# Eight banks of PSUM shared out anew in a fused attention and feed-forward kernel

## Chip, cores and metric

One core of one Trainium2 chip runs the whole program. The metric is the device time of one execution in microseconds (us); the time before is the median of three runs. A profile is one more execution, taken with the hardware profiler on.

## What is computed

Input is `x` of 128 sequences x 64 steps x 256 features (fp32), and one condition vector of 256 for each sequence. The reference, cut to what matters:

```python
# layer 0: a gated recurrence over the 64 steps, then a quantised feed-forward (256 -> 704 -> 256)
def step(h, z_t):
    gate = sigmoid(h @ Wh.T + z_t @ Wz.T + b)
    h_new = tanh(h * leak + gate * z_t)
    return h_new, h_new
...
h = _act_fake_quant(silu(gate) * up, clip_down[0])        # needs the largest |h| of all tokens
x = x + h @ _weight_fake_quant(w_down).T                  # "down projection"
# layer 1: a block in hyperbolic space with adaptive layer norm, 16 heads of 16
xn = layer_norm(logmap0(x));  xm = expmap0(xn * (1 + sc_msa) + sh_msa)
q, k, v = (_to_heads(plin(xm, w, b)) for w, b in ...)
attn = softmax(q k / sqrt(16))
attn_out = plin(_from_heads(expmap0(attn @ v)), w_o, b_o)
x2 = mobius_add(x, expmap0(g_msa * logmap0(attn_out)))
xn = layer_norm(logmap0(x2)); xm = expmap0(xn * (1 + sc_mlp) + sh_mlp)
ff = plin(plin(xm, w_f1, b_f1), w_f2, b_f2)               # "feed-forward"
y = mobius_add(x2, expmap0(g_mlp * logmap0(ff)))
# layer 1: a linear layer on values rounded to fp6 in blocks of 32
out = x + mx_quantize(y) @ mx_quantize(weight).T + bias   # "fp6 linear"
```

## The kernel before

The 8192 tokens are 64 tiles of 128 tokens; four tiles are a group, so there are 16 groups, and a group is worked on as two pairs of tiles.

Up to about 310 us the recurrence runs, then the wide half of the quantised feed-forward, whose result goes to DRAM because its scale needs the largest value of all tokens. From there on one fused part (`fused`) takes the groups through everything else. Its main loop issues, for a step `k`:

- `tail(k)`: the end of a residual step for the attention of group `k` and the feed-forward of group `k - LM` (LM = 3) together: `tail_coeffs` (from L745) is a chain of some 35 small VectorE (DVE) instructions on 128 x 8 numbers with powers on GpSimd (POOL, `rsqrt`, L632), then `combine` (L789).
- `norms(k)`: the layer norms for the feed-forward of group `k` and the attention of group `k + LA` (LA = 5) together: `ln_coeffs` (from L658) is a second chain of that kind, then `modulate` (L712 to L717), a sum of squares on ScalarE (ACT, L601), and `clip_ball` (L610, L612), which scales the result.
- `fp6(k - LM)`: rounding, transposition (`turn`, L92), copy to SBUF (L1077), product (L1081, L1083), sum with the residual (L1086).
- `mlp(k)`: transposition, a split in two parts (L1021, L1022), product in three passes (L1026, L1029), read out by DVE (L1032) and ACT (L1035), then L1041.
- `attention(k + LA)`: transposition and projection to q, k, v (`qk`, L905, L908, copied by L910), norms of the heads (L912 to L925), their scaling on POOL (L934, L938), transposition and scores (`sc`, L959), exponentials (L967), attention times values (`ao`, L974, read out by L978 and L979), transposition, copy (L995) and output projection (L1000, read out by L1004), then `tail_sums` (L601 and L729).
- `front(k + LA + 1)`: the down projection of layer 0 for a later group (`dn`, L872, read out by L874), sum with the input `xr` (L875), statistics for its norm (L695, L696).

TensorE (PE) writes only to PSUM, which has eight banks of 128 x 512 fp32 numbers. A tile of PSUM is a whole bank, and `bank(tag)` (L591) takes the next of the tag's buffers: 2 for `qk`, 2 for `sc`, 1 each for `ao`, `ml`, `fp`, `dn`, as CFG (L46) says. A tag with one buffer can be written again only when its last reader, on DVE or ACT, is done.

What stands in which order is not written out by hand. The program is built under

```python
    with _tile.TileContext(nc, schedule_with_timeline_sim=True) as tc:
```

so a planner takes the instructions as issued, with the loop's order as their priority, follows its own estimate of when operands and buffers become free, and lays down a queue for each engine. On the chip each engine works through its queue in that order and waits on semaphores. The functions marked `@first` (`radial`, `ln_coeffs`, `tail_coeffs`) have a higher priority. All loads and stores are issued from one queue, that of SyncE (SP, `move`, L567).

Of the kernel before, what the change touches and what calls it, by code (L numbers as in the profile page):

```python
# [11 lines left out]
F32 = mybir.dt.float32  # L12
# [10 lines left out]
P = 128  # L23
# [19 lines left out]
NG = NT // GN  # L43
AR = 8
TS = 4
CFG = {'rnd': 'S', 'ef': 8, 'fill': {'x1a': 'V', 'mod0': 'V'}, 'hold': [3, 0], 'mk': 3, 'mv': 6, 'xs': 3, 'la': 3, 'sb': 7, 'qks': 'GGGG', 'deq': 'VV', 'first': 1000, 'hb': 2, 'q_h': 'P', 'q_x1': 'P', 'q_xr': 'P', 'q_ot': 'P', 'q_out': 'P', 'q_ada': 'P', 'room': [[0.3, 0.3, 0.55], [0.5, 0.4, 0.2]], 'qv': 64, 'p1': 'GVGVGVGV', 'x1': 3, 'u1': 16, 'u2': 6, 'qkv': 2, 'sq': 1, 'uT1': 2, 'uT2': 2, 'qM': 2, 'kT': 2, 'e': 4, 'oT': 1, 'yT': 1, 'hq': 2, 'hl': 2, 'xr': 1, 'ot': 2, 'ada00': 2, 'ada02': 2, 'ada10': 2, 'ada12': 4, 'dn': 1, 'qk': 2, 'sc': 2, 'ao': 1, 'ml': 1, 'fp': 1, 'mod0': 'GGGV', 'mod1': 'VVVV', 'sqm0': 'SSSS', 'sqm1': 'SSSS', 'su0': 'VVVV', 'su1': 'VGVG', 'q8': 'GGGGGG', 'hqc': 'SSSVVV', 'qm': 'SSSS', 'x1a': 'GV', 'gate0': 'GGGG', 'gate1': 'GGGG', 'yb': 'GG', 'va': 'GGGG', 'sqt': 'SSSS', 'sqg': 'SSSS', 'sqo': 'SSVS', 'f2e': 'SSSS', 'early': 0, 'q8f': 'VVVVVV', 'hqf': 'SSSVVV', 'fl': 1, 'un': 2, 'jsu': 1, 'LA': 5, 'LM': 3, 'tl': 6, 'ord': 1, 'xt': 3, 'q_xt': 'P'}  # L46
GT = 4
NGR = NTILE // GT

LA, LM = CFG["LA"], CFG["LM"]  # L50

# [19 lines left out]
def tile_kernel(ctx, tc, a, out):  # L71
# [64 lines left out]
    with ExitStack() as l0:  # L136
# [15 lines left out]
        with ExitStack() as sc_:  # L152
# [260 lines left out]
            for n in range(T // TS):  # L413
# [5 lines left out]
                for i in range(TS):  # L419
# [22 lines left out]
                    with tc.issue_after(lv.ins), tc.issue_after(ls.ins), tc.issue_after(lp.ins):  # L442
                        next(ahead, None)
                        for q in range(2):
                            if t < CFG["hold"][q]:
                                continue
                            left[q] = [min(l, 0.0) + r for l, r in zip(left[q], CFG["room"][q])]
                            while min(left[q]) > 0:
# [25 lines left out]
        for b0 in range(0, B, NBB):  # L474
            for c in range(2):

                q8 = xp.tile([P, NBB, T], I8, name="q8", tag="q8")
                src = hsT[:, c, :, b0 : b0 + NBB].rearrange("p t b -> p b t")
                if b0 < CFG["qv"]:
                    V.tensor_scalar(q8, src, isx, None, ALU.mult)  # L480
# [16 lines left out]
        def h_chunk(pg, pu, j, at, dst):  # L497
# [3 lines left out]
            cnt[0] += 1  # L501
            if CFG["p1"][cnt[0] % 8] == "G":
                uv = fw.tile([P, GN], F32, name="uv", tag="uv")
# [39 lines left out]
def fused(ctx, tc, a, out_tok, x_tok, L):  # L543
    nc = tc.nc
    V, S, G_, PE = nc.vector, nc.scalar, nc.gpsimd, nc.tensor
# [10 lines left out]
    ps = ctx.enter_context(tc.tile_pool(name="fps", bufs=1, space=PSUM))  # L556
# [9 lines left out]
    def move(key, out, in_):  # L566
        Q[CFG["q_" + key]].dma_start(out=out, in_=in_)  # L567

# [19 lines left out]
            es = CFG["fill"].get(key, es)  # L588
        return es[g % len(es)]

    def bank(tag):  # L591
        return ps.tile([P, 512], F32, name=tag, tag=tag, bufs=CFG[tag])

    def big(tag, shape, dt=F32):
        return pl.tile(shape, dt, name=tag, tag=tag, bufs=CFG[tag])
# [248 lines left out]
    def front(i):  # L844
# [4 lines left out]
        for h2 in pairs:  # L849
            pr = i0 // 2 + h2  # L850
            early = pr < CFG["early"]
            grp = pr // 2
            hs_ = slice((grp % 2) * 64, (grp % 2) * 64 + 64)
            hl = hls.pop(0)
            hq = big("hq", [P, 6, 2 * P], BF16)
            q8 = big("hb", [P, 6, 2 * P], I8)

            for e, r, j in runs("q8f" if early else "q8", hs_):
                scale(e, q8[r, j, :], hl[r, j, :], cu[r])
            for e, r, j in runs("hqf" if early else "hqc", hs_):  # L860
                if e == "V":
                    V.tensor_copy(hq[r, j, :], q8[r, j, :])
                else:
                    S.copy(hq[r, j, :], q8[r, j, :])
            load_h(pr + CFG["hl"])
            xr = big("xr", [P, 2, D])
            move("xr", out=xr, in_=x_tok[:, i0 + 2 * h2 : i0 + 2 * h2 + 2, :])
            py = bank("dn")
            for i in range(2):
                for j in range(6):  # L870
                    r = slice(0, P) if j < 5 else hs_
                    PE.matmul(py[:, i * D : (i + 1) * D], lhsT=hq[r, j, i * P : (i + 1) * P], rhs=wdT[r, j, :],  # L872
                              start=(j == 0), stop=(j == 5))
            V.tensor_tensor(x1.t[h2], two(py), bc_out(sdh, 2), ALU.mult)  # L874
            ENG[pick("x1a", h2)].tensor_tensor(x1.t[h2], x1.t[h2], xr, ALU.add)  # L875
            for g in (2 * h2, 2 * h2 + 1):
                stats(mv1[:, g, :], x1[g], 1)
            move("x1", out=x1_d[:, i0 + 2 * h2 : i0 + 2 * h2 + 2, :], in_=x1.t[h2])

    def attention(i, u, sums):  # L880
# [4 lines left out]
        for h2 in pairs:  # L885
# [3 lines left out]

            uT = big("uT1", [P, 2, 2, 2 * P], F32R)  # L890
            pt = bank("qk")
            for c in range(2):
                po = pt[:, c * 256 : (c + 1) * 256].rearrange("p (s g t) -> p s g t", s=2, g=2)
# [5 lines left out]
            for xy in range(2):  # L899
                cs = slice(xy * P, (xy + 1) * P)  # L900
                for lo, hi in ((0, 512), (512, 768)):
                    pm = bank("qk")
                    n_ = hi - lo
                    o3 = slice(0, 3) if lo == 0 else slice(32, 35)
                    PE.matmul(pm[:, :n_], lhsT=ones3[o3, :], rhs=rows3[o3, :n_], start=True, stop=False)  # L905
                    for k in range(2):
                        for q, (w, z) in enumerate(PASSES):
                            PE.matmul(pm[:, :n_], lhsT=uT[:, z, k, cs], rhs=wqkv[:, w, k, lo:hi],  # L908
                                      start=False, stop=(k == 1 and q == 2))
                    S.copy(qkv[:, xy, lo:hi], pm[:, :n_])  # L910
                sq = big("sq", [P, 3 * D])
                S.activation(sq, qkv[:, xy, :], AF.Square)  # L912
                V.tensor_reduce(nh[:, xy * 48 : (xy + 1) * 48], sq.rearrange("p (h d) -> p h d", d=HD),  # L913
                                AX.X, ALU.add)
# [302 lines left out]
```

## Time and profile before

| | |
|---|---|
| runs of before | 1414.75, 1404.55, 1413.27 us: median 1413.27 |
| profiled execution | 1410.42 us, span 1408.5 us, granted clock 0.859 |
| busy, share of the span | PE 84%, DVE 81%, POOL 59%, ACT 58% |
| DMA | 163.64 MB, mean 116 GB/s |
| 300 to 420 us (fused part begins, attention of the first groups) | PE busy 78.3 of 120.0 us |
| 540 to 680 us | PE 129.7, DVE 121.5 of 140.0 us |
| 820 to 960 us | PE 120.7, DVE 129.7 of 140.0 us |
| 1300 to 1408.5 us (last groups run out) | PE 68.2, DVE 66.1 of 108.5 us |

The span is the time from the first to the last instruction. "Busy" is the time in which an engine has an instruction under way. "Granted clock" is the share of TensorE's full clock that the throttle lets through. Where a row shows "A <- B", A waited until B was done. Where a group of instructions is named, its name is that of the tile that is written and those that are read, without buffer numbers (`ao<-va,e`).

### The profile page before, as it was taken

Reading aid. Unit: us, or ns where it says so; the run is one execution under the profiler, and the core shown is the slowest. Engines: PE = TensorE matmul, PEld = TensorE weight load, DVE = VectorE, ACT = ScalarE, POOL = GpSimd, SP = SyncE. Lnnn points to the kernel's source line nnn. Section 1 sums busy time; section 2 is a strip of 40 time slices with the busy share of each in tenths; the row PEclk is TensorE's granted clock in tenths of the full one; section 3 lists DMA queues with packets and bytes.
Section 4 is the critical chain, followed back from the end, with each engine's and each line's share of the span. In section 5 each row is a group of like instructions: output and inputs, shape, how many; then the busy total and the mean of one; then the engine's idle time right before and its main releaser. Section 6 shows DMA issues by size and latency. Waiting matters only on the chain.

```text
span 1408.5 us, 23861 instructions
## 1 busy us (share of the span) xinstructions
PE 1183.5 (84%) x7372; PEld 748.0 (53%) x7380; DVE 1144.8 (81%) x3604; ACT 815.5 (58%) x2363; POOL 836.6 (59%) x1043
## 2 busy tenths in 40 slices
PE   7999977974699988999889988799996999785655
PEld 4656542322466655656556565556664666553433
DVE  5666669986687988979989789979889888788863
ACT  2545447972377766667656666667765756643331
POOL 3111108865688769776685776867758764645541
PEclk9999979985599987989879899889987969976675
DMA  7113145779534234341354231532314132222111
GB/s 230 53 53 92 59 198 206 273 253 301 166 118 127 94 103 134 109 135 46 101 151 146 81 115 43 158 116 77 102 39 136 49 119 68 82 73 93 60 45 45
DMA packets 119304, 163.64 MB, mean 116 GB/s; under 512 B 10885, under 2 KB 72074, under 8 KB 119178
## 3 DMA queue, kind: packets, MB, share of 16 engines
q1 hardware_dynamic: 119178, 162.13, 36.4%
q8 instruction: 58, 0.95, 0.3%
q14 instruction: 68, 0.56, 0.1%
HBM read 115.94 MB, written 46.14 MB: 115 GB/s over the span
## 4 chain that ended last, share of the span: by engine, by line
DVE 40%; PE 35%; POOL 10%; DMA 7%; ACT 4%; issue 4%; SPq 0%; POOLq 0%; DVEq 0%; ACTq 0%
DMA ada<-ada_d 4%; PE pg L426 4%; PE qk L908 4%; PE fp L1083 4%; DVE u L789 4%; PE pg L407 3%; PE sc L959 3%; PE ml L1029 2%; PE ao L974 2%; DVE nh L913 2%; DVE bn L695 2%; DVE u L716 2%; DVE junk L735 2%; DVE u L610 2%; DVE u L1041 2%
## 5 line engine op out<-in xcount | busy, mean ns | idle before, releaser
L601 ACT ACTIVATE junk<-u 128x256 bf16<-128x256 f32 x432 | 182.2, 424 | 143.0 <-DVE u L717 46.2
L908 PE MATMUL qk<-wqkv,uT 128*128 128x512 f32 (+1 forms) x768 | 199.4, 390 | 6.3 <-DVE uT L898 3.5
L729 POOL TENSOR_TENSOR u<-u,ada 128x256 f32<-128x256 f32 x128 | 101.1, 792 | 91.7 <-ACT junk L601 88.6
L908 PEld LDWEIGHTS qk<-wqkv,uT 128*128 128x128 f32 x768 | 129.9, 207 | 46.5 <-issue 12.4
L959 PE MATMUL sc<-qM,kT 64*64 64x256 f32 x1024 | 126.7, 437 | 9.7 <-ACT kT L949 6.1
L974 PE MATMUL ao<-va,e 128*64 128x34 f32 x2048 | 93.3, 248 | 35.4 <-DVE u L979 15.3
L1029 PE MATMUL ml<-wm,uT 128*128 128x512 f32 x384 | 122.6, 457 | 0.0
L974 PEld LDWEIGHTS ao<-va,e 128*64 128x64 f32 x2048 | 83.5, 163 | 62.5 <-issue 36.3
L608 ACT ACTIVATE qM<-sc,mhead 128x256 f32<-128x256 f32 x256 | 101.3, 492 | 21.3 <-PE sc L92 21.1
L872 PE MATMUL dn<-wdT,hq 128*128 128x256 bf16 (+1 forms) x384 | 72.3, 315 | 41.3 <-DVE x L874 16.5
L938 POOL TENSOR_TENSOR va<-qkv,comb 64x256 f32<-64x256 f32 x128 | 87.2, 682 | 30.1 <-PE ao L974 24.3
L1029 PEld LDWEIGHTS ml<-wm,uT 128*128 128x128 f32 x384 | 75.5, 212 | 53.5 <-issue 35.0
L505 POOL TENSOR_TENSOR hv<-uv,sil 128x512 f32<-128x512 f32 x44 | 57.4, 1308 | 70.8 <-DVE am L508 52.2
L1083 PE MATMUL fp<-wfT,yT 128*128 128x256 f32 x256 | 92.6, 491 | 0.0
L967 ACT ACTIVATE e<-sc 128x512 f32<-128x512 f32 x128 | 73.3, 596 | 24.5 <-PE sc L959 15.1
L910 ACT COPY qkv<-qk 128x512 f32<-128x512 f32 (+1 forms) x128 | 61.3, 498 | 44.4 <-PE qk L908 43.6
L601 ACT ACTIVATION_READ_ACCUMULATOR junk<-u 128x1 f32 x432 | 86.1, 199 | 0.0
L426 PE MATMUL pg<-hsT,WT 128*128 128x128 f32 x504 | 76.3, 292 | 10.8 <-ACT hsT L438 10.4
L934 POOL TENSOR_TENSOR qkv<-qkv,comb 128x512 f32<-128x512 f32 x64 | 70.4, 1117 | 23.7 <-DVE comb L925 9.3
L426 PEld LDWEIGHTS pg<-hsT,WT 128*128 128x128 f32 x504 | 66.1, 195 | 33.3 <-ACT hsT L438 31.1
L959 PEld LDWEIGHTS sc<-qM,kT 64*64 64x64 f32 x1024 | 55.5, 147 | 48.3 <-issue 17.3
L612 POOL TENSOR_SCALAR hb<-hl,cu 128x1280 int8<-128x1280 f32 x64 | 64.8, 1018 | 23.0 <-DMA hl<-h_d 14.3
(282 smaller groups left out, 3129.7 us busy)
## 6 DMA issues: line engine op xcount, KB each, us to landing
ada<-ada_d SPq DMA_DIRECT2D x128, 256.0 KB, 3.5
h_d<-hv SPq DMA_DIRECT2D x80, 256.0 KB, 2.1
hl<-h_d SPq DMA_DIRECT2D x32, 640.0 KB, 5.1
ada<-ada_d SPq DMA_DIRECT2D x128, 128.0 KB, 2.6
xt<-in_xT_dram SPq DMA_DIRECT2D x16, 512.0 KB, 4.1
xr<-in_x_dram SPq DMA_DIRECT2D x32, 256.0 KB, 3.7
x_d<-x SPq DMA_DIRECT2D x32, 256.0 KB, 2.4
xt<-x_d SPq DMA_DIRECT2D x32, 256.0 KB, 2.7
```

Source lines behind the costliest of these rows:

```text
L426: lp = PE.matmul(pg[c][:, st], lhsT=WT[:, k, c * P : (c + 1) * P], rhs=hp[:, k, :], start=False, stop=False, skip_group_check=True)
L601: S.activation(junk, src, AF.Square, accum_out=acc)
L608: S.activation(dst, src, AF.Copy, scale=by)
L729: ENG[pick(f"gate{which}", g)].tensor_tensor(av, av, gb, ALU.mult)
L872: PE.matmul(py[:, i * D : (i + 1) * D], lhsT=hq[r, j, i * P : (i + 1) * P], rhs=wdT[r, j, :], start=(j == 0), stop=(j == 5))
L908: PE.matmul(pm[:, :n_], lhsT=uT[:, z, k, cs], rhs=wqkv[:, w, k, lo:hi], start=False, stop=(k == 1 and q == 2))
L938: ENG[pick("va", g)].tensor_tensor(va[r, :, s, 0:HD], qkv[r, xy, 512:768].rearrange("p (h d) -> p h d", d=HD), bc_in(comb[r, xy * 48 + 32 ...
L959: PE.matmul(sc[rr][s * T : (s + 1) * T, c * 256 : (c + 1) * 256].rearrange("p (v t) -> p v t", v=4), lhsT=kTs[xy][r, c, s * T : (s + 1) * ...
L967: S.activation(e.rearrange("p c v t -> p (c v t)"), sc[rr], AF.Exp, scale=1.0 / math.sqrt(HD))
L974: PE.matmul(pv[xy * T : (xy + 1) * T, hh], lhsT=E[2 * xy + hh // 4][:, c, hh % 4, :], rhs=vas[(2 * h2 + xy) % 4][:, c * 8 + hh], start=Tru ...
L1029: PE.matmul(pm, lhsT=uT[:, z, k, i * P : (i + 1) * P], rhs=wm[:, w, k, :], start=False, stop=(k == 1 and q == 2))
L1083: PE.matmul(o, lhsT=yT[:, 2 * i + c, :], rhs=wfT[:, c, :], start=False, stop=(c == 1))
```

## The change

`ao` gets two buffers instead of one. The tags `ml`, `fp` and `dn` become one tag, `m`, with two buffers, which the three take in turn, in the order in which the planner places them. Eight banks are in use as before. The two added lines move the code below them by two lines; line numbers in this document are those of the kernel before.

```diff
-CFG = {... 'ada12': 4, 'dn': 1, 'qk': 2, 'sc': 2, 'ao': 1, 'ml': 1, 'fp': 1, 'mod0': 'GGGV', ...}
+CFG = {... 'ada12': 4, 'qk': 2, 'sc': 2, 'ao': 2, 'm': 2, 'mod0': 'GGGV', ...}
...
-    def bank(tag):
-        return ps.tile([P, 512], F32, name=tag, tag=tag, bufs=CFG[tag])
+    def bank(name):
+
+        tag = "m" if name in ("ml", "fp", "dn") else name
+        return ps.tile([P, 512], F32, name=name, tag=tag, bufs=CFG[tag])
```

## Prediction

> **What bounds the kernel now.** I read the page first: TensorE and VectorE carry almost the same load.
>
> ```profile
> PE 1183.5 (84%) x7372; PEld 748.0 (53%) x7380; DVE 1144.8 (81%) x3604; ACT 815.5 (58%) x2363; POOL 836.6 (59%) x1043
> ```
>
> Then I cut the fused part of the trace where one group's norm chain gives way to the next: L658 (`tln`) is the first instruction of `ln_coeffs`, it starts once per group, at 576.3 us for one group and at 1083.1 us for the one eight groups later. The stretches show span, then busy time (and instructions) of PE, PEld, DVE, ACT, POOL, then the granted clock.
>
> ```profile
> 312.00:576.30 264.30, 215.82 (x1551) 138.50 (x1552) 215.99 (x651) 156.07 (x427) 194.60 (x255) 0.81 0.49 147
> 576.30:1083.10 506.80, 446.67 (x3180) 297.26 (x3178) 449.58 (x1457) 323.89 (x995) 358.50 (x445) 0.89 0.35 106
> 1083.10:1408.50 325.40, 252.52 (x1417) 164.34 (x1415) 247.70 (x936) 157.16 (x496) 171.81 (x212) 0.77 0.22 69
> ```
>
> The middle stage takes 506.8 / 8 = 63.35 us a group, with PE at 88% and DVE at 89%: no engine has much room, and both must run beside each other all the time. How that is done shows when the middle stage is cut into the time from a group's L658 to its last scaling at L610 (the norm chain, after which `mlp` and `attention` of that group may begin):
>
> ```profile
> 662.50:725.70 63.20, 50.52 (x346) 33.37 (x342) 61.51 (x194) 38.13 (x116) 47.10 (x59) 0.89 0.43 129
> 704.00:764.00 60.00, 53.53 (x377) 35.52 (x377) 51.29 (x157) 37.81 (x116) 45.23 (x56) 0.88 0.46 142
> 773.00:829.00 56.00, 52.71 (x348) 33.99 (x347) 42.70 (x118) 35.81 (x107) 42.10 (x53) 0.91 0.31 98
> ```
>
> The norm chain is DVE and POOL work, but PE is busy for 50.5 to 53.5 us of it: the order has put matmuls of other groups beside it. The waits that the change is aimed at are in the list of who waited for whom (total us, times, longest), PE alone:
>
> ```profile
> PE dn L872 <- DVE x L874: 16.5, 9, 4.0
> PE ao L974 <- DVE u L979: 15.3, 6, 6.8
> ...
> PE ao L974 <- DVE u L1004: 11.2, 6, 3.3
> ...
> PE ml L92 <- ACT u L1035: 7.0, 5, 3.1
> ...
> PE ao L92 <- DVE u L1004: 6.7, 3, 4.3
> ...
> PE ml L1026 <- ACT u L1035: 4.9, 6, 1.8
> ```
>
> Each is a matmul that waits for its tag's only bank to be read out, 61.6 us together over the whole run.
>
> **What the change does, part by part.** No instruction is added or removed: counts per line are equal in the two programs.
>
> (1) The second `ao` bank. The waits on L979 and L1004 (15.3 + 11.2 + 6.7 = 33.2 us) can go. With two banks, what comes after c = 0 of the attention's result is c = 1 or a transposition, and neither waits for DVE.
>
> (2) `dn`, `ml`, `fp` lose a bank between them. The waits of `dn` and `ml` on their own bank (16.5 + 7.0 + 4.9 = 28.4 us) can go, but now each can wait for another's reader. The nearest rows are these same waits: from -28.4 us, all gone, to +28.4 us, as many again. I take 0 for it: an eviction reads the bank for 0.39 to 0.68 us (L1035, L874) and in the changed order other matmuls mostly stand between.
>
> (3) The order. A planner lays out each engine's queue when the program is built, and it follows which bank is free. So every queue changes, SP's loads too, and this part decides. I read the changed program's order for eight middle groups; from the third on they repeat almost instruction by instruction. I cut each group at the same two places, L658 and the last L610 (numbered as before), counted what stands between on each engine, and priced it with the mean of its row between 620 and 1240 us. Rows added up overstate time, since instructions overlap: from 300 us on they sum to 1015 us for PE, where the profile has 919 us busy, and to 1086 for DVE, where it has 922. So I scale PE by 0.90 and DVE by 0.85. Check on the order of before: its eight middle groups then sum to PE 448.8 and DVE 460.2 us, beside 446.67 and 449.58 in the profile.
>
> Stretch N, L658 to last L610, in the changed order. PE: 32 score matmuls x 0.227 + 16 transpositions x 0.150 + 34 attention matmuls x 0.082 = 12.4 us. DVE: two L913 x 0.80, eight L789 x 0.48, ten L716/L717 x 0.50, two each of L1070, L1057, L979, L695 at 0.65, 0.57, 0.35, 0.35, and some 80 others of 0.13 to 0.58 (17.9 us) = 32.2 us. ACT 24.9, POOL 30.3 (four L632 x 2.03, eight L938 x 0.70, four L934 x 1.1).
>
> Stretch M, last L610 to the next L658. PE: 48 L908 x 0.229, 24 L1029 x 0.280, 32 transpositions x 0.168, 8 L1083 x 0.592, 8 L1000 x 0.454, 24 `dn` x 0.147, 16 bias matmuls (5.1 in all), 30 attention matmuls x 0.082 = 42.5 us. DVE 24.2, ACT 25.4, POOL 15.4.
>
> The same count in the order of before gives PE 42.8 to 49.9 us beside the norm chain in six of seven groups (32.9 in the other). The changed order keeps 12.4. So N is bound by DVE with PE nearly idle, M by PE with DVE half idle, and the two alternate: M's first matmuls (`ml` and `qk` transpositions) need L610 of N; N's L658 needs the statistics of `dn`, which stands two thirds into M, and a few places behind L658 DVE's queue holds L1086, which waits for the last `fp` product, 3.4 us of PE ahead of M's end. All small DVE work of `ln_coeffs` and `tail_coeffs` is queued behind that L1086, and POOL's L632 and the scalings wait for it.
>
> Length of N: from 32.2 us (DVE never waits) to 40.3 (plus the four L632 results once each: 2.96 + 1.67 + 1.75 + 1.73). I take the densest DVE seen in a stretch, 61.51 / 63.20 = 0.973: 33.1 us. It is near what the chain takes with little beside it, early in the fused part:
>
> ```profile
> 327.80:360.90 33.10, 10.78 (x44) 5.00 (x43) 25.71 (x76) 6.13 (x16) 21.91 (x25) 0.50 0.99 290
> 347.00:380.00 33.00, 20.84 (x75) 11.54 (x75) 22.01 (x73) 9.92 (x24) 20.50 (x25) 0.60 0.75 216
> ```
>
> Length of M: from 42.5 us to 47.1 (at the 90% that PE reaches from 543 to 1226 us). I take the densest PE seen, 52.71 / 56.00 = 0.94: 45.2 us. The late `dn` also moves the load of `xr` (one buffer): L874 0.67, L875 on POOL 1.33, `xr` load 3.7, L875 on DVE 0.97, two L695 and L696 1.0 = 7.7 us from the last `dn` to L658. 14.0 us of matmuls stand behind `dn` in M, so this costs nothing; without that cover it is 7.7 us a group.
>
> Sum: 33.1 + 45.2 = 78.3 us a group beside 63.35, so 8 x 14.95 = +119.6 us; ends 74.7 and 87.4, +91 and +192. Fill and drain (589.7 us) I leave as they are: the changed order moves 67 us of PE work into the fill, which has 48.5 us of idle PE, and takes 57 from the drain. Bounds for that: 0 to +22 us (the larger engine sum of the two stages goes from 489.5 to 508.1, at the 1.205 us per us that they take now), and -30 us if all of (1) falls there. From the profiled execution's 1410.4 us (span 1408.5; median of three 1413.3): 1410.4 + 119.6 = 1530.
>
> The clock. In the row at 327.8 us PE was busy for a third of the time, with pauses, and the granted clock was 0.50; in the middle stage it is 0.89. N of the changed order has the same PE load as that row. The Trainium skill, TensorE: Matmul & The Clock Gate, HAM oscillation, says that an idle gap of over some 3.4 us puts the array back to half clock. By that rule each M starts cold and loses an estimated 1.7 us, 8 x 1.7 = 14 us, and the sum would be 1544. The same section says that PSUM double-buffering brought no further gain on its kernel, which speaks against a gain from this change; by the row of PE's waits alone the gain would be up to 61.6 us.
>
> **Rivals.**
> Softer alternation: N starts while M's last matmuls run. For it: 14.0 us stand behind `dn`, and only 7.7 are needed. Against it: the place of L1086 in DVE's queue. It saves 14.0 - 7.7 = 6.3 us a group: 72.0 us, 1410.4 + 8 x 8.65 = 1480.
> Faster: the waits on banks go and the stretches run into each other, since PE may run ahead where nothing holds it. For it: 61.6 us of waits, and equal sums (PE 54.9, DVE 56.4 a group, against 63.35). Price: the middle stage can shrink to DVE's 449.6 / 0.973 = 462 us, -45: 1365. It decides from the point where over 15 us a group of N's DVE work lies beside M's matmuls. Against it: L610 holds all of M's first matmuls.
> No change: about 15 us a group overlap after all, so that what is gained on banks is lost in the order: 1410. The equal work in both programs speaks for it, the 12.4 us against 43 to 50 against it.
>
> **How the numbers follow.** Forecast 0.63, softer alternation 0.20, no change 0.07, faster 0.10. Three runs of before spread over 0.7%, so some 1% can be told from no change. The time is that of the forecast, 1530. The range runs from 1430, between the softer case and no change, to 1620, the end of 87.4 us a group (1602) with the 22 us of fill and drain taken almost whole. Faster 0.10, within 1% 0.07, slower 0.83.
>
> **What would show it.** Right: L658 comes every 75 to 87 us in the middle stage; between L658 and the last L610 PE is busy for some 12 us of 33, with a granted clock well under 0.89; PE's waits on L979 and L1004 for `ao` are gone; PE's longest waits are on L610 and on `sc`. Wrong: L658 every 63 us or less, or PE busy for over 25 us between L658 and L610.

## Result and profile after

The changed kernel takes 1603.17 us (median of 4 runs, 1602.06 to 1606.32) where the kernel before takes 1409.66 us (4 runs): ratio 1.1376, 95% interval 1.1323 to 1.143. The forecast was 1530 us in a range of 1430 to 1620: right in direction and cause, with 119.6 us where 193.5 were to come.

Line numbers from here on are those of the changed kernel, two higher than before from L591 on (L658 is now L660, L610 is L612, L974 is L976). The page shows that no engine has more to do. DVE, ACT and POOL are busy for within 11 us of what they were; PE's busy time grew by 85 us with the same 7372 instructions, at a mean granted clock of 0.797 instead of 0.859.

```profile
PE 1268.4 (79%) x7372; PEld 793.5 (49%) x7380; DVE 1155.8 (72%) x3604; ACT 822.3 (51%) x2363; POOL 828.5 (52%) x1043
```

The fused part, cut at the same groups' L660 as before (columns: span, then busy time and instructions of PE, PEld, DVE, ACT, POOL, granted clock, DMA share, GB/s):

```profile
317.00:666.60 349.60, 284.80 (x2096) 185.06 (x2096) 262.21 (x822) 204.54 (x590) 228.78 (x278) 0.83 0.39 117
666.60:1308.10 641.50, 507.63 (x3063) 331.15 (x3062) 453.03 (x1421) 318.70 (x949) 341.86 (x430) 0.74 0.27 83
1308.10:1604.50 296.40, 204.75 (x979) 128.38 (x977) 206.02 (x798) 119.38 (x376) 142.80 (x179) 0.73 0.22 67
```

The eight middle groups take 641.5 us instead of 506.8 (80.2 a group, +134.7). The fill, the time before them, takes 349.6 instead of 259.3 counted from 317 us (+90.3). The drain, the time after them, takes 296.4 instead of 325.4 (-29.0). Together that is the +196 of the span. The fill of before from the same start:

```profile
317.00:576.30 259.30, 212.48 (x1539) 137.11 (x1539) 212.00 (x646) 154.78 (x425) 191.25 (x229) 0.81 0.49 145
```

PE is at 79% and DVE at 71% of the middle stage: neither is the bound any more. They take turns. Two groups cut at the last L612 show it, in each first the norm stretch N, then the matmul stretch M:

```profile
972.90:1017.80 44.90, 26.61 (x164) 15.26 (x163) 35.11 (x115) 20.49 (x62) 28.82 (x35) 0.57 0.27 85
1017.80:1057.30 39.50, 37.74 (x220) 26.56 (x220) 22.74 (x65) 19.51 (x58) 14.16 (x19) 0.89 0.25 81
1057.30:1103.20 45.90, 27.32 (x166) 15.41 (x165) 35.92 (x115) 20.54 (x62) 29.37 (x36) 0.58 0.29 89
1103.20:1143.20 40.00, 38.40 (x222) 26.63 (x221) 23.37 (x64) 19.42 (x59) 14.71 (x19) 0.89 0.17 56
```

In M, PE is busy for 96% and DVE for 58%. In N, DVE is busy for 78%, and PE runs at little over half clock (0.57 and 0.58). Over the eight middle groups N lasted 33.9 to 45.9 us (mean 40.8) and M 35.1 to 41.2 (mean 39.4).

PE's waits, as before (total us, times, longest):

```profile
PE sc L961 <- ACT kT L951: 70.7, 33, 8.5
PE sc L92 <- POOL qkv L936: 58.9, 23, 6.8
PE ml L92 <- DVE u L612: 35.6, 6, 14.8
PE ao L976 <- ACT e L969: 20.5, 10, 3.0
...
PE dn L874 <- DVE x L876: 7.1, 1, 7.1
PE ml L1028 <- ACT u L1037: 5.3, 4, 2.5
PE ao L92 <- DVE u L981: 5.3, 3, 2.7
...
PE fp L1083 <- DVE ot L1088: 4.3, 4, 2.8
```

The waits on banks did shrink: those of `ao` from 33.2 us to 7.9 (5.3 here, 2.6 further down the list), those of the three on the shared tag to 21.1 (16.7 here, 4.4 of `fp` further down) from 31.1 (the forecast's 28.4, and 2.7 of `fp` on its own reader, L1086 of before). One row of before (line numbers of before) that the forecast didn't count went too. The first product L1026 of `ml` reads constants only, so what it waited for was the one bank, until L1022 had read the transposed values out of it:

```profile
PE ml L1026 <- DVE uT L1022: 17.1, 8, 4.0
```

The first three rows of after took the place of these waits: scores that wait for the attention's scaling on ACT and POOL, and `ml`, which waits for the norm chain. In the list of before, the first has 6.1 us, the second isn't in it, and the third has 0.5.

### The profile page after: what moved, and what is told of

The parts are those of the page before. It is cut to its first block, busy times and chain, and to the rows that moved or that the text cites. A ratio compares the mean times of both kernels' runs of the same rounds, so it can differ in the third digit from the quotient of the medians.

```text
span 1604.5 us, 23919 instructions
## 1 busy us (share of the span) xinstructions
PE 1268.4 (79%) x7372; PEld 793.5 (49%) x7380; DVE 1155.8 (72%) x3604; ACT 822.3 (51%) x2363; POOL 828.5 (52%) x1043
## 4 chain that ended last, share of the span: by engine, by line
PE 39%; DVE 32%; POOL 11%; DMA 8%; ACT 5%; issue 4%; SPq 0%; POOLq 0%; DVEq 0%; ACTq 0%
PE ml L1031 7%; DMA ada<-ada_d 6%; PE qk L910 5%; PE pg L426 4%; DVE u L791 3%; PE pg L407 3%; PE ao L1002 3%; PE sc L961 3%; PE ao L976 2%; DVE u L718 2%; DVE u L719 2%; PE fp L1085 2%; DVE u L1043 2%; DVE hq L864 1%; POOL r L634 1%
## 5 line engine op out<-in xcount | busy, mean ns | idle before, releaser
L961 PE MATMUL sc<-qM,kT 64*64 64x256 f32 x1024 | 191.0, 552 | 81.1 <-ACT kT L951 70.7
L910 PE MATMUL qk<-wqkv,uT 128*128 128x512 f32 (+1 forms) x768 | 183.8, 367 | 13.6 <-DVE uT L900 10.6
L961 PEld LDWEIGHTS sc<-qM,kT 64*64 64x64 f32 x1024 | 78.9, 184 | 156.7 <-ACT kT L951 93.3
L910 PEld LDWEIGHTS qk<-wqkv,uT 128*128 128x128 f32 x768 | 120.7, 194 | 51.2 <-DVE uT L900 13.8
L976 PEld LDWEIGHTS ao<-va,e 128*64 128x64 f32 x2048 | 108.5, 191 | 64.2 <-issue 29.2
L976 PE MATMUL ao<-va,e 128*64 128x34 f32 x2048 | 119.2, 274 | 23.3 <-ACT e L969 20.5
L1031 PE MATMUL ml<-wm,uT 128*128 128x512 f32 x384 | 132.9, 477 | 2.3 <-ACT uT L1023 1.8
L610 ACT ACTIVATE qM<-sc,mhead 128x256 f32<-128x256 f32 x256 | 101.2, 477 | 17.0 <-PE sc L92 17.0
L92 PE MATMUL sc<-ident,qkv 128*128 128x128 f32 x256 | 57.6, 365 | 59.0 <-POOL qkv L936 58.9
L1085 PE MATMUL fp<-wfT,yT 128*128 128x256 f32 x256 | 81.9, 448 | 2.0 <-ACT yT L1079 1.7
L915 DVE TENSOR_REDUCE nh<-sq 128x48 f32<-128x768 f32 x64 | 60.4, 943 | 31.7 <-ACT sq L914 31.5
L426 PEld LDWEIGHTS pg<-hsT,WT 128*128 128x128 f32 x504 | 66.1, 195 | 33.1 <-ACT hsT L438 30.8
```

Source lines behind the costliest of these rows:

```text
L426: lp = PE.matmul(pg[c][:, st], lhsT=WT[:, k, c * P : (c + 1) * P], rhs=hp[:, k, :], start=False, stop=False, skip_group_check=True)
L610: S.activation(dst, src, AF.Copy, scale=by)
L961: PE.matmul(sc[rr][s * T : (s + 1) * T, c * 256 : (c + 1) * 256].rearrange("p (v t) -> p v t", v=4), lhsT=kTs[xy][r, c, s * T : (s + 1) * ...
L976: PE.matmul(pv[xy * T : (xy + 1) * T, hh], lhsT=E[2 * xy + hh // 4][:, c, hh % 4, :], rhs=vas[(2 * h2 + xy) % 4][:, c * 8 + hh], start=Tru ...
L1031: PE.matmul(pm, lhsT=uT[:, z, k, i * P : (i + 1) * P], rhs=wm[:, w, k, :], start=False, stop=(k == 1 and q == 2))
L1085: PE.matmul(o, lhsT=yT[:, 2 * i + c, :], rhs=wfT[:, c, :], start=False, stop=(c == 1))
```

## Why the order changed: a theory

The order in which the program takes its banks of `ml`, `fp` and `dn` on PE, a group to a line (from one L660 to the next):

```
before:  ml fp ml fp ml fp fp ml dn ml ml dn ml ml ml
         ml fp ml ml fp dn fp
         fp dn fp fp ml fp fp ml ml dn ml dn ml
after:   ml ml ml ml ml ml dn dn fp fp fp fp
         ml ml ml ml ml ml dn dn fp fp fp fp
         ml ml ml ml ml ml dn dn fp fp fp fp
```

After the change, ten successive groups, two of them in the fill, have `ml` first and then `dn`. The theory: tiles of one tag get its banks in the order in which the program issues them, and the planner can't swap them (so it isn't its placing that decides their turns, as the section on the change has it). The loop issues `mlp(k)` before `front(k + 6)`. So with a common tag, the down projection of group `k + 6` stands behind the last `ml` product of group `k`. `norms(k + 1)` needs the statistics of that down projection, because one `ln_coeffs` does both groups. And `mlp(k + 1)` needs `norms(k + 1)`. That closes a ring, ml, dn, norms, ml, that goes round once a group: no `mlp` can lie beside the norms of its successor. The rivals: too few banks in the shared tag, the second `ao` bank, or any sharing as such.

## The experiments

Ratios are to the kernel before, run on the same chip. All edits are to the changed kernel unless a diff shows another start.

**Which tags may share.** First, three tags on three banks, `ao` back to one:

```diff
-'ao': 2, 'm': 2
+'ao': 1, 'm': 3
```

> Theory (tied order): tiles that share a tag get their banks in the order in which they are issued, so the down projection of group k+6 comes after the feed-forward of group k, the norms of the next group come after it, and the next feed-forward after those. The number of banks is not the cause. With ao 1 and three banks for the shared tag the time stays near that of the changed kernel: 1590 to 1620 us, with L658 every 78 to 82 us and PE busy below 30 us of each norm chain. Rival (too few banks: three tags on two banks wait for each other): the third bank takes those waits away, 1410 to 1470 us. Second rival (the second bank of ao makes the order bad): ao is back to 1, about 1410 us.

1588.85 us, ratio 1.1282 (1.1217 to 1.1348), 79.9 us a middle group. One more bank for the three and one fewer for `ao` bring back under 1%; the time lies 1 us below the range expected. PE is busy for 25 to 28 us of each N. The second `ao` bank isn't the cause, nor is the shared tag short of banks.

Then `dn` on a bank of its own, and `ml` and `fp` together on one:

```diff
-'ao': 2, 'm': 2
+'ao': 2, 'dn': 1, 'm': 1
-        tag = "m" if name in ("ml", "fp", "dn") else name
+        tag = "m" if name in ("ml", "fp") else name
```

> ao 2; the down projection has its own bank again; feed-forward and fp6 linear share one. Theory: the tie between feed-forward and down projection is gone, so the order mixes the groups again: 1385 to 1430 us, the gain or loss against before under 2%. Rival (sharing itself costs, by bank waits): feed-forward and fp6 have half the banks they have in the changed kernel, so at least 1500 us.

1501.67 us, ratio 1.0664 (1.0611 to 1.0717): half of the loss is gone. The theory's range is missed, and the time lies in the rival's (at least 1500). This edit also took a bank away, and PE's waits show that as a new cost:

```profile
PE fp L92 <- DVE ot L1088: 17.8, 10, 3.4
...
PE ml L1028 <- ACT u L1037: 13.1, 11, 2.2
...
PE fp L92 <- ACT u L1037: 12.0, 10, 2.8
...
PE ml L92 <- ACT u L1037: 8.6, 5, 2.2
```

These are 51.5 us of waits of `ml` and `fp` on their only bank; the rows of before that answer to them sum to 14.6 (7.0 + 4.9 + 2.7). That is not all of the 88 us by which the profiled span grew: 26 are in the eight middle groups and 60 in the drain, and the rest of their cause isn't shown. The same split with two banks, and `ao` back to one:

```diff
-'ao': 2, 'm': 2
+'ao': 1, 'dn': 1, 'm': 2
-        tag = "m" if name in ("ml", "fp", "dn") else name
+        tag = "m" if name in ("ml", "fp") else name
```

> ao 1; the down projection has its own bank; feed-forward and fp6 linear take two in turn. So only two tags are joined, none loses a bank, and the down projection is not tied to the feed-forward. Theory (the tie between down projection and feed-forward costs some 190 us, and the run with one bank for feed-forward and fp6 was at 1502 us for want of banks): 1390 to 1430 us. Rival (joining feed-forward and fp6 costs by itself, since fp6 of group k-3 then stands in line with the feed-forward of group k): 1450 to 1510 us.

1409.03 us, ratio 1.0008 (0.9985 to 1.0031). It differs from the kernel before only in that `ml` and `fp` take two banks in turn. That orders their work too (from the first `fp` of the program to its last `ml`, four banks of `fp` and six of `ml` take turns), and it moves work: the middle groups take 467.6 us instead of 506.8, the drain 366.6 instead of 325.4. In sum it costs and brings nothing. Sharing as such is not the cause. The counterpart, with `ml` and `dn` together and `fp` on its own:

```diff
-'ao': 2, 'm': 2
+'ao': 1, 'm': 2, 'fp': 1
-        tag = "m" if name in ("ml", "fp", "dn") else name
+        tag = "m" if name in ("ml", "dn") else name
```

> Only ml and dn share the tag (two banks in turn), fp and ao keep their own bank as in the kernel before. If the loss comes from dn being tied behind ml by the common tag, this alone brings all of it back: 1580 to 1625 us, a group every 79 to 82 us in the middle. If all three of ml, fp and dn have to share, or the second ao bank takes part, it stays below 1500 us.

1589.51 us, ratio 1.1276 (1.1211 to 1.1342). The whole difference to the run above is whether `ml` shares with `fp` or with `dn`, with as many banks in both. Its middle stage is close to the changed kernel's 80.2, 658.0 / 8 = 82.3 us a group (just above the 79 to 82 expected) at a clock of 0.73:

```profile
668.90:1326.90 658.00, 512.20 (x3095) 333.69 (x3096) 454.53 (x1406) 323.11 (x957) 344.20 (x435) 0.73 0.27 82
```

**The order without the banks.** The kernel before with its own banks; only the planner is told that `dn` goes behind the last `ml` product issued:

```diff
+    last = []
...
-                    PE.matmul(py[:, i * D : (i + 1) * D], lhsT=hq[r, j, i * P : (i + 1) * P], rhs=wdT[r, j, :],
+                    with tc.issue_after(last[-1].ins) if last else nullcontext():
+                        PE.matmul(py[:, i * D : (i + 1) * D], lhsT=hq[r, j, i * P : (i + 1) * P], rhs=wdT[r, j, :],
...
-                        PE.matmul(pm, lhsT=uT[:, z, k, i * P : (i + 1) * P], rhs=wm[:, w, k, :],
+                        lm = PE.matmul(pm, lhsT=uT[:, z, k, i * P : (i + 1) * P], rhs=wm[:, w, k, :],
...
+                last.append(lm)
```

> The kernel before with all its banks (ao 1, and one each), where only the planner is told to put the down projection behind the last product of the feed-forward that was issued before it. Theory: the order alternates as in the changed kernel and the time is 1560 to 1620 us, without any change of banks. Rival (banks): as before, 1400 to 1420 us.

1606.91 us, ratio 1.1411 (1.1348 to 1.1474):

```profile
678.30:1324.80 646.50, 484.61 (x3122) 324.73 (x3123) 441.65 (x1437) 332.77 (x975) 343.72 (x434) 0.75 0.28 86
```

80.8 us a group. The order alone gives the whole loss, with every bank where it was. In this run the last of a group's two residual sums (L1086 of before) starts 21 us or more ahead of the next norm chain, and not behind its first instruction: the place of L1086 isn't needed for the loss.

**Slack in the ring.** The changed kernel with its banks, and `front` one loop step earlier, so that `dn` stands behind `mlp` one group sooner than its norms need it:

```diff
-'fl': 1
+'fl': 2
```

> The changed kernel's banks (ao 2, three tags on two), but front is issued one loop step earlier (fl 2), so that the norms need a down projection that stands behind the feed-forward of the group before the last. Theory: the same tie now has a group of slack; the norm chain runs beside the feed-forward again, PE is busy for over 40 us of it, and most of the loss is gone: 1430 to 1490 us (three buffers of x1 may hold it back somewhat). Rival (banks): nothing about the banks changes, 1600 us.

1480.06 us, ratio 1.051 (1.0454 to 1.0565), 68.4 us a middle group. The tie remains but has a group of slack, and 123 us come back; PE is busy for 54 us or more of each norm chain in the middle (over 40 was expected). What holds the other 73 us was asked with one more buffer of `x1`, which `front` writes:

```diff
-'fl': 1, ... 'x1': 3
+'fl': 2, ... 'x1': 4
```

> The changed kernel with front one loop step earlier and four buffers of x1 instead of three. If x1's three buffers are what holds the step-earlier front back at 1480 us, this gives 1420 to 1465 us. If what is left is the tie itself (dn still stands behind ml, only of an earlier group), it stays at 1470 to 1495 us.

1489.49 us, ratio 1.0573 (1.0496 to 1.065): `x1` isn't it. That the tie itself costs the rest fits, but is not shown.

**The length of N.** In N the chain of waits (start, us, what) passes through two loads of `ada`, the modulation's factors (L567 issues them), and then through 3.9 us of scores that stand on PE ahead of M's first `ml`:

```profile
998.39 3.36 DMA ada<-ada_d
...
1006.52 3.62 DMA ada<-ada_d
...
1010.21 0.74 POOL u L715
...
1012.82 1.97 PE sc L961 x8
...
1015.36 1.90 PE sc L961 x8
1017.25 0.41 PE ml L92
```

A load of `ada` can start only when one of its tag's two buffers is read out by the modulation before. The middle stage of the changed kernel waits 64.0 us for them:

```profile
POOL u L715 <- DMA ada<-ada_d: 34.0, 8, 5.2
...
DVE u L718 <- DMA ada<-ada_d: 30.0, 12, 4.1
```

The same two rows are 20.5 us in the middle stage of before:

```profile
DVE u L716 <- DMA ada<-ada_d: 12.7, 9, 3.4
...
POOL u L713 <- DMA ada<-ada_d: 7.8, 7, 2.4
```

The changed kernel with twice as many buffers for the two tags that the norms load; three others give up the room:

```diff
-'ada00': 2, 'ada02': 2, 'ada10': 2, 'ada12': 4, 'ot': 2
+'ada00': 4, 'ada02': 1, 'ada10': 4, 'ada12': 2, 'ot': 1
```

> The changed kernel with four buffers each for the modulation rows that the norms load (ada00 and ada10, two before); to make room in SBUF ada12 goes from 4 to 2, ada02 from 2 to 1, ot from 2 to 1. The norm chain measured 41 to 46 us where 33.1 was forecast, and the chain of waits shows two ada loads of 3.4 and 3.6 us in it. Theory (the loads are the mis-sized term): the wait of L716 and L713 on ada is gone, the chain is 4 to 8 us shorter in some ten groups, 1525 to 1565 us. Rival (the loads are hidden beside DVE's and ACT's own work): 1590 to 1610 us. The buffers that were taken away could add a little in either case.

1531.71 us, ratio 1.0891 (1.0858 to 1.0924), 74.0 us a middle group. N lasts 32.7 to 37.0 us there (mean 34.3 instead of 40.8); M is unchanged (mean 39.6 beside 39.4). One of its N stretches:

```profile
938.40:973.20 34.80, 25.13 (x212) 16.27 (x210) 29.50 (x101) 17.36 (x57) 25.05 (x32) 0.55 0.42 113
```

**A better version.** If `dn` shares with `fp`, it stands behind `fp6(k - 3)`, which is long done, and no ring closes. That frees a bank, for `ao` or for `ml`. First for `ao`:

```diff
-'ao': 2, 'm': 2
+'ao': 2, 'ml': 1, 'fd': 1
-        tag = "m" if name in ("ml", "fp", "dn") else name
+        tag = "fd" if name in ("fp", "dn") else name
```

> ao 2; feed-forward has its own bank; fp6 linear and down projection share one. It is the nearest to the second ao bank alone. Theory: feed-forward and down projection are not tied, so the order mixes the groups; what the second ao bank takes away (33 us of waits) comes against waits of fp6 on the down projection: 1390 to 1440 us. Rival (the second ao bank spoils the order by itself): 1480 us or more.

1388.06 us, ratio 0.9872 (0.9848 to 0.9895). And with the bank given to `ml`:

```diff
-'ao': 2, 'm': 2
+'ao': 1, 'ml': 2, 'fd': 1
-        tag = "m" if name in ("ml", "fp", "dn") else name
+        tag = "fd" if name in ("fp", "dn") else name
```

> ao 1; feed-forward has two banks of its own; fp6 linear and down projection share one. The feed-forward's waits for its bank were 11.9 us on PE, and DVE and ACT waited for its products too. Theory: the groups stay mixed and the feed-forward is quicker: 1385 to 1420 us. Rival (fp6 and the down projection wait for each other): 1430 to 1480 us.

1381.97 us, ratio 0.9844 (0.9799 to 0.989). Both are faster than the kernel before, by 1.3% and 1.6%, and each lies a few us below its expected range. Their intervals overlap, so the runs don't tell which is better; nor do they part what the bank brings from what joining `fp` and `dn` brings. In the profile of the second, the middle stage is 487.7 / 8 = 61.0 us a group, with DVE at 93%:

```profile
580.90:1068.60 487.70, 444.50 (x3112) 290.13 (x3111) 453.54 (x1443) 324.26 (x995) 352.25 (x437) 0.89 0.36 109
```

So the eight banks had up to 25 us (1406.69 to 1381.97) to give, but not with `dn` behind `ml`.

## Why the prediction was right, and by how much not

(1) The second `ao` bank: right. The waits of 33.2 us went to 7.9. In the changed kernel PE waits for the norms instead; where the ring is open, the version with the second bank (`ao` 2 and `fd`) is 1.3% faster than before.

(2) The shared banks: taken as 0, and right: waits on them fell by 10 us (and by the 17.1 of L1026, which the forecast left out), and joining `ml` and `fp` alone moved the time by 0.08%.

(3) The order decides: right, and shown by the run that changes the order alone. The forecast read the alternation off the program and found that N needs `dn` and M needs L612. It didn't see why `dn` stood there, that the shared tag had put it behind `ml`, and so it offered the place of L1086 in DVE's queue as what keeps the stretches apart. The ring is enough for that, as the two runs with `ml` and `fp` or `ml` and `dn` together show; with the order alone, L1086 stood elsewhere and the loss was whole.

The two terms of a group were both mis-sized, in opposite ways. N was put at 33.1 us (end 40.3) and lasted 40.8 on the mean. (The row at 327.8 us, which was to back the 33.1, holds the norms of one attention group alone: 76 DVE instructions, where N has 115.) The missing step is the loads of `ada`: in the changed order a load has nothing to hide behind, two of them (3.36 and 3.62 us) stand in the chain, and with more buffers N is 34.3 us. M was put at 45.2 us (end 42.5) and lasted 39.4: its last matmuls run on into the next N. Of PE's costliest groups of instructions between 1057.3 and 1103.2 us, three are the attention's own, and the next is 12 of L910, the projection of the stretch before:

```profile
L961 PE MATMUL sc<-qM,kT 64*64 64x256 f32 x64 | 14.3, 644 | 8.3 <-ACT kT L951 7.8 <-ACT e L969 0.5
L976 PE MATMUL ao<-va,e 128*64 128x34 f32 x68 | 5.1, 301 | 2.8 <-ACT e L969 2.8
L92 PE MATMUL sc<-ident,qkv 128*128 128x128 f32 x16 | 4.5, 434 | 7.5 <-POOL qkv L936 7.5
L910 PE MATMUL qk<-wqkv,uT 128*128 128x512 f32 (+1 forms) x12 | 2.6, 355 | 0.0
```

(Busy us and mean ns of one stand behind the count; the forecast's 32 score and 34 attention matmuls make two records each.) Those of L910 run in the first 4.7 us of N, where PE is busy for 3.45 us. That is some of the softer alternation. The three upper rows are the work that the forecast counted into N, at 12.4 us; they take 23.9, because a score matmul lasts 644 ns at half clock where the middle stage of before has 442. Of the prediction's signs, L658 every 75 to 87 us came on the mean (72.7 to 86.2). The half clock spoils another test that it set itself: PE busy for over 25 us in N was to speak against it, and the two N stretches above show 26.6 and 27.3 (23.8 to 28.9 over the eight groups). Beside the L910, the work was as forecast and only its time was not; a count of instructions would have been the better test. That the sum of both terms, 78.3 us a group, came near the 80.2 measured is luck: the two errors nearly cancel.

The step that failed is fill and drain: left as they are, with bounds of -30 to +22 us, they gave +61.3. The work was read rightly: 67 us of PE work were to move into the fill, and PE's busy time there grew by 72.3. But it was put at no cost into 48.5 us of idle PE, as if it could run beside what was there. The program's order shows ten groups with `dn` behind `ml`, not eight; the two in the fill take 96.3 and 84.6 us where those of before take 43.6 and 47.4, which is the +90. The drain gave 29 back. The range to 1620 held because the middle groups stayed at +134.7, well under their end of +192.

Of the softer alternation (1480) the kernel has the 3.45 us a group above, of 6.3 that the rival counted on. The faster rival had the right price in view (bank waits), and the versions with `fd` collect up to 25 us; no change (1410) is what `ml` and `fp` on two banks give.

The clock fell as weighed: in the two N stretches above it is 0.57 and 0.58. It falls after a pause and comes back late:

```profile
1057.30:1062.00 4.70, 3.45 (x16) 2.02 (x15) 4.51 (x20) 2.31 (x6) 1.37 (x2) 1.00 0.59 184
1062.00:1064.00 2.00, 0.00 (x0) 0.00 (x0) 1.49 (x5) 0.41 (x3) 2.00 (x1) 1.00 0.39 136
1064.00:1065.00 1.00, 0.00 (x0) 0.00 (x0) 0.78 (x1) 0.19 (x1) 1.00 (x2) 0.61 0.49 90
...
1012.00:1026.00 14.00, 13.59 (x95) 8.30 (x93) 5.54 (x17) 3.99 (x12) 4.83 (x8) 0.50 0.12 39
1026.70:1057.30 30.60, 28.84 (x148) 19.95 (x148) 19.82 (x56) 17.95 (x53) 12.64 (x16) 1.00 0.32 105
```

PE's last matmul ahead of the pause ends at 1060.7 us, and the clock halves just after 1064, as the idle gap of some 3.4 us that the forecast quotes would have it. In the group before, PE is busy for 13.59 of 14 us and still has half clock; M's first 8.9 us (1017.8 to 1026.7) run so. That can cost up to 4.4 us a group, 36 us in eight, where the estimate from the Trainium skill (TensorE: Matmul & The Clock Gate, HAM oscillation) was 14. The same page says, under What's actually happening, that some 3.4 us of sustained work bring the full clock back; by the busy time in this row that doesn't hold here, and the measurement decides. The forecast left the clock out of M and still had M too long, so how much of N and M the clock costs was not measured by itself.

## What to carry to other kernels

Buffers that share a tag were handed out in the order issued in every run above, so a shared tag is an order between otherwise independent work; before joining two, ask whether one is issued after the other and needed by its next round. Join what is finished long before (here `dn` with `fp`), and give the freed bank to the one that waits. When an order is read off a built program, count over how many groups it holds, fill included, and list every load that loses its cover.

## What the hardware showed

The granted clock has two values in these rows, 1.00 and 0.50 (means lie between). It stayed at 0.50 through 14 us in which PE was busy for 97%. The work in that time began with the score and attention matmuls (64x256 and 128x34), and the full clock came back 4.2 us after the first wide `ml` product (128x512) started. In two other groups of the same execution it came back at 709.2 and 784.3 us, 2.5 and 5.7 us after the first product of the output projection (128x256). Whether the shapes keep it down, and how many us are needed, was not tried. The stretch at half clock that ends at 1026.7 us lasts 47.79 us and the one at full clock behind it 37.55: 14 and 11 times 3.413 us.
